# A four-layer attention stack: expert blocks with first weights copied by VectorE and a turned first product, and a third layer on multiplied weights

## The chip, the cores and the metric

The kernel runs on one core of a Trainium2 chip. The core has a matrix engine (TensorE, PE in the profile; PEld is its weight loading), a vector engine (VectorE, DVE), a scalar engine (ScalarE, ACT), GpSimd (POOL) and SyncE (SP), which here only issues transfers. Each engine works through its own instruction stream in order and waits on semaphores for the others. The metric is the time of one execution on the device in microseconds (us), as the median of several runs.

## The reference

Four layers follow each other on 64 sequences of 64 tokens of width 128 (4096 tokens), all in float32: an attention layer with relative positions, an encoder-decoder layer, a "vision" layer, and a layer with two attentions and a mixture of experts. The change touches the last two. Cut to what matters:

```python
# third layer: per sequence, one pooled vision vector gates the tokens
vision_pooled = jnp.mean(vision_feat, axis=1, keepdims=True)
text_proj   = einsum('blh,oh->blo', text_feat, Wt) + bt
vision_proj = einsum('bkh,oh->bko', vision_pooled, Wv) + bv
agreement   = sum(text_proj * vision_proj, axis=-1)
# (third round) weights = softmax over the sequence of 2*agreement
weighted = weights * vision_proj
gate  = sigmoid(text_proj @ Wg_t.T + weighted @ Wg_v.T + bg)
fused = text_feat + gate * weighted          # then a layer norm

# end of the fourth layer: 8 experts, each token goes to its best 2
h = _ln(x, ln_g, ln_b)
vals, idx = top_k(h @ rw.T + rb, 2);  gates = softmax(vals)
h1 = gelu(hf @ fc1_w[e].T + fc1_b[e])        # 128 -> 512
eo = h1 @ fc2_w[e].T + fc2_b[e]              # 512 -> 128
out = x + sum_over_2(gates * eo[idx])
```

## The kernel before, in words

Tokens are worked on in eight groups of 512. The first layer is written with a fixed order of instructions; everything after it (`other_layers`) is a set of Python generators that a small loop, `drive`, advances in turn, so that instructions of several groups are traced interleaved. Behind that stands the library's planner: it takes the traced order as priority and puts on each engine's stream whatever its own timing model holds to be ready first, within the number of buffers of each tile name. An engine then runs its stream strictly in the planned order.

Per group the later layers are `self1`, `cross1`, `forward1`, `layer2` (the vision layer), `self3` and `cross3`. `cross3` ends in `router`: it finds both experts of each token and a row number for each, and writes the normalised row of each token (`zx`, 128 values and four more columns: the token's number, its first expert, and two numbers from which the gate is made) twice into a DRAM table `hrows`, by eight indirect writes of GpSimd per group. Then the router computes the gate-weighted second bias of the experts (tiles `gates`, `pgt`, `T`, and a product with `fc2b`) and adds it to `x`.

`experts` works through that table in blocks of 128 rows of one expert: 47 blocks for the first five groups and 31 for the other three, 78 in all. It is traced beside the last routers, from the point at which the last attention has issued its exponentials, and takes the rest of the program. For block t one round of its loop traces:

- `load(t+6)`: SP reads the row number into a register and loads 128 rows (eight buffers);
- `first(t)`: PE reads the expert's offset into a register; one product of 512 columns with the rows as stationary operand (`f<-fcw,vp` in the profile, two passes); VectorE copies the result out of PSUM (`h<-f`);
- `hidden_turned(t-1)`: four PE transposes (`ht<-ident,h`), then four ScalarE gelus with the bias of the hidden unit as per-partition operand;
- `second(t-3)`: four accumulated products (`f<-fcw,s`, two passes each), VectorE multiplies by the gate (`km<-f,m`), GpSimd scatters the rows to `yrows`;
- `turn(t+2)`: one PE transpose of the loaded rows (`xt`), ScalarE scale and shift (`vp<-xt,cols`), and four one-column VectorE operations for gate and target row (`m`, `tob`).

The buffers that count: six result tiles `you`, sixteen `tob`, four `h1`, seven PSUM banks. When a half is done, `summed` adds the two result rows of each token to `x`: per group one GpSimd addition and one VectorE addition of 128x512, then the store. For five groups this happens among the blocks of the second half, for the last three after the last block.

All instructions go through one helper, so the profile gives line 74 for nearly all; tiles tell them apart.

Of the kernel before, what the change touches and what calls it, by code (L numbers as in the profile page):

```python
# [16 lines left out]
P = 128  # L17
B = 64
S = 64
# [14 lines left out]
ROWW = D + 4  # L34
# [60 lines left out]
def kernel(ctx: ExitStack, tc: tile.TileContext, a: dict, out: bass.AP):  # L95
# [573 lines left out]
    def experts():  # L669
# [7 lines left out]
        def table(h):  # L677
# [11 lines left out]
            for e in range(1, NE):  # L689
# [19 lines left out]
                tab[:, 1, :], eb[0:1, :], float(NE - 1), 1024.0, ALU.min, ALU.mult  # L709
# [28 lines left out]

        def turn(i):
            h, j = slot(i)  # L740
            b = held[i]
            rows_in = b["in"]
            pt = pmm("xt")
            nc.tensor.transpose(pt[:, 0:P], rows_in[:, 0:D], ident)
            b["x"] = wtile([P, P], "vp", 3)
            nc.scalar.activation(b["x"], pt[:, 0:P], AF.Identity, scale=col("moe_g"), bias=col("moe_b"))

            m = wtile([P, 3], "m", 12)
            b["to"] = wtile([P, 1], "tob", 16, U32)
            nc.vector.tensor_tensor(  # L750
                m[:, 0:1], rows_in[:, D + 1 : D + 2], tables[h][1][:, j : j + 1], ALU.is_equal
            )
            nc.vector.tensor_tensor(
                m[:, 2:3], rows_in[:, D + 1 : D + 2], tables[h][1][:, j : j + 1], ALU.not_equal
            )
            nc.vector.tensor_scalar(
                b["to"], m[:, 2:3], float(PARTS[h] * T), rows_in[:, D : D + 1], ALU.mult, ALU.add
            )
            nc.vector.tensor_scalar(
                m[:, 1:2], m[:, 0:1], rows_in[:, D + 3 : D + 4], rows_in[:, D + 2 : D + 3], ALU.mult, ALU.add  # L760
            )
            b["gate"] = m[:, 1:2]

        def first(i):
            h, j = slot(i)
            b = held[i]
            b["e"] = value(nc.tensor, tables[h][0][0:1, 1, j : j + 1], (NE - 1) * 1024)
            ps = pmm("f1")
            nc.tensor.matmul(ps, lhsT=b["x"], rhs=fcw[:, bass.ds(b["e"], 512)], start=True, stop=True)
            b["u"] = wtile([P, 512], "h1", 4)  # L770
            nc.vector.tensor_copy(b["u"], ps)

        def hidden_turned(i):
            h, j = slot(i)
            b = held[i]
            pt = pmm("ht")
            for c in range(NFC):
                nc.tensor.transpose(pt[:, c * P : (c + 1) * P], b["u"][:, c * P : (c + 1) * P], ident)
            b["h"] = wtile([P, 512], "s", 10)
            for c in range(NFC):  # L780
                nc.scalar.activation(
                    b["h"][:, c * P : (c + 1) * P], pt[:, c * P : (c + 1) * P], AF.Gelu,
                    bias=tables[h][2][:, c, j : j + 1],
                )
# [3 lines left out]
        def second(i):  # L788
# [3 lines left out]
            for c in range(NFC):  # L792
                nc.tensor.matmul(
                    po[:, 0:D], lhsT=b["h"][:, c * P : (c + 1) * P],
                    rhs=fcw[:, bass.ds(b["e"] + (512 + c * D), D)],
                    start=(c == 0), stop=(c == NFC - 1),
                )
            y = you[i % 6]
            nc.vector.tensor_scalar(y, po[:, 0:D], b["gate"], None, ALU.mult)
# [24 lines left out]
        def summed(g, ys):  # L824

            o = wtile([P, NBLK, D], "o", 2)
            nc.gpsimd.tensor_tensor(o, ys[0], v3(xs[g][:, :], NBLK), ALU.add)
            nc.vector.tensor_tensor(o, o, ys[1], ALU.add)
            nc.sync.dma_start(out[g * NBLK : (g + 1) * NBLK].rearrange("k p d -> p k d"), o)
# [9 lines left out]
        you = [room[:, 8 * ROWW + k * D : 8 * ROWW + (k + 1) * D] for k in range(6)]  # L839
        total = LAST[-1]  # L840
        reads = {}
        for t in range(-6, total + 3):
# [3 lines left out]
            if h < NH and h not in tables:  # L846
                yield from table(h)
            if t + 6 < total:
                load(t + 6)
            if 0 <= t < total:  # L850
                first(t)
            if 0 <= t - 1 < total:
                hidden_turned(t - 1)
            if 0 <= t - 3 < total:
                second(t - 3)
# [3 lines left out]
            for h in range(NH - 1):  # L859
                gl, at = divmod(t - 3 - LAST[h] - 4, 4)  # L860
                if 0 <= gl < PARTS[h]:
                    g = sum(PARTS[:h]) + gl
                    if at == 0:
                        reads[g] = read(g)
                    if at == 2:
                        summed(g, reads.pop(g))
# [9 lines left out]
    def other_layers(ends):  # L876
# [4 lines left out]
        fc2b = wtile([NE, D], "fc2b", 1)  # L881
# [4 lines left out]
        nc.scalar.dma_start(fc2b, a["fc2b"])  # L886
# [13 lines left out]
        toki = wtile([P, max(PARTS) * NBLK], "toki", 1, I32)  # L900
# [41 lines left out]
        def small_heads(qT, kvT, wq, wk, wv, wo, scale, bias=None, maskb=None, then=None, bare=None, row_behind=None):  # L942
# [147 lines left out]
            scores(1)  # L1090
            yield
            turn_weights(0)
            yield
            turn_weights(1)
            yield
            turn_weights(2)
            products(0)
            yield
# [51 lines left out]

        ff = {}

        def cross1(g):
            x = xs[g]
            if g == 1:
                value_biases()
            if g == 0:
# [11 lines left out]
                bare=lambda: transpose4(ct.rearrange("p b i -> p (b i)")),  # L1169
# [16 lines left out]
        def layer2(g):  # L1186
            x = xs[g]
            load_expert(g)
            ct = ctx_of(g, 2)
            wt, wv, wgt, wgv = (w2l[:, i, :] for i in range(4))  # L1190
            xT = turned(x)
            pool = wtile([P, NB], "pool", 2)
            nc.vector.tensor_reduce(pool, ct, axis=AX.X, op=ALU.add)
            nc.vector.tensor_scalar(pool, pool, 1.0 / S, None, ALU.mult)
            yield
            pv = extra("pv")
            nc.tensor.matmul(pv[0:NB, 0:D], lhsT=pool, rhs=wv, start=True, stop=True)
            vp = wtile([P, D], "vp", 3)[0:NB, :]
            nc.vector.tensor_tensor(vp, pv[0:NB, 0:D], row("l2_bv")[0:NB, :], ALU.add)
            pv2 = extra("pv2")  # L1200
            nc.tensor.matmul(pv2[:, 0:NB], lhsT=wv, rhs=pool, start=True, stop=True)
            vpT = wtile([P, NB], "vpT", 2)
            nc.vector.tensor_scalar(vpT, pv2[:, 0:NB], col("bv"), None, ALU.add)
            ptp = project(xT, wt)
            tpT = wtile([P, T], "T", 4)
            nc.scalar.activation(tpT, ptp, AF.Identity, bias=col("bt"))
            yield

            pa = pmm("pa")
            nc.tensor.matmul(pa[0:NB, :], lhsT=vpT, rhs=tpT, start=True, stop=True)  # L1210
            eye = last(ident[0:NB, 0:NB], S)
            rwd = wtile([NB, NB, S], "rwd", 2)
            nc.vector.tensor_tensor(rwd, v3(pa[0:NB, :], NB), eye, ALU.mult)
# [4 lines left out]
            am = wtile([NB, 2], "am", 2)  # L1218
# [9 lines left out]
            pw = pmm("pw")  # L1228
            nc.tensor.matmul(pw, lhsT=vp, rhs=rw2, start=True, stop=True)
            wvT = wtile([P, T], "T", 4)  # L1230
            nc.scalar.copy(wvT, pw)
            pw2 = pmm("pw2")
            for k in range(NBLK):
                nc.tensor.matmul(
                    pw2[:, k * P : (k + 1) * P], lhsT=rw2[:, k * P : (k + 1) * P], rhs=vp, start=True, stop=True
# [3 lines left out]
            yield  # L1239
            pg = tokens_by(lambda c: (tpT, wvT)[c], lambda c: (wgt, wgv)[c], 2)  # L1240
            gt = wtile([P, T], "z", 3)
            nc.vector.tensor_tensor(v3(gt[:, :], NBLK), v3(pg[:, :], NBLK), mid(row("l2_bg"), NBLK), ALU.add)
# [74 lines left out]
        def router(g, hT, x, zx):  # L1317
# [59 lines left out]
            nc.vector.tensor_tensor(e2, e2, g1, ALU.mult)  # L1377
# [6 lines left out]
            nc.vector.tensor_copy(meta(2), e2)  # L1384
            nc.vector.tensor_tensor(meta(3), g1, e2, ALU.subtract)
# [17 lines left out]
            yield  # L1403

            gates = wtile([P, NBLK, NE], "gates", 3)
            nc.vector.tensor_tensor(gates, hots[0], last(g1[:, :], NE), ALU.mult)
            nc.vector.tensor_tensor(hots[1], hots[1], last(e2[:, :], NE), ALU.mult)
            nc.vector.tensor_tensor(gates, gates, hots[1], ALU.add)
            yield
            pgt = extra("pgt")  # L1410
            for k in range(NBLK):
                nc.tensor.transpose(pgt[0:NE, k * P : (k + 1) * P], gates[:, k, :], ident)
            gT = wtile([NE, T], "T", 4)
            nc.vector.tensor_copy(gT, pgt[0:NE, :])
            yield
            pb = tokens_by(lambda c: gT, lambda c: fc2b)
            nc.vector.tensor_tensor(x, pb, x, ALU.add)

# [26 lines left out]
    fcw = mtile([P, NE * 1024], "fcw")  # L1445

    def load_expert(e):
        nc.scalar.dma_start(fcw[:, e * 1024 : e * 1024 + 512], a["fc1"][e])
        nc.scalar.dma_start(
            v3(fcw[:, e * 1024 + 512 : (e + 1) * 1024], NFC), a["fc2"][e].rearrange("(f c) d -> c f d", c=P)  # L1450
        )
# [87 lines left out]
```

## Time and profile before

| | |
|---|---|
| median of 3 runs (lowest to highest) | 1729.73 us (1729.42 to 1736.37) |
| the profiled execution, its span | 1729.11 us, 1727.3 us |
| busy: PE, PEld, DVE, ACT, POOL | 1589.0, 1148.9, 1209.1, 1002.0, 913.4 us |
| first layer | about 0 to 727 us |
| layers two to four | about 727 to 1513 us |
| expert blocks, first product to last scatter | 1513.2 to 1712.1 us |
| last reads, sums and stores | 1713.5 us to the end |

Engines overlap, so busy times do not add up to the span. "Idle before" an instruction names the engine or transfer that released it. In a line such as `f<-fcw,s 128*128 x8` the output tile stands left of the arrow and the inputs right of it, digits left out; f is any of the tiles f1 and f2.

### The profile page before, as it was taken

The numbers are of one execution on the slowest core, as the hardware profiler recorded it, in microseconds if no ns is written. First come the engines' busy times: TensorE is split into PE (matmuls) and PEld (weight loads), VectorE is DVE, ScalarE is ACT, GpSimd is POOL, SyncE is SP. The second block draws the span as 40 slices with busy tenths as digits, with TensorE's granted clock in tenths as the row PEclk, the third lists the DMA queues.
The fourth block names the chain that finished last, engine by engine and source line by source line (L and its number), as shares of the span: only waits on it lengthen the run. The fifth ranks groups of instructions, "written<-read, shape, count | busy, mean of one in ns | idle before, by whom it ended". The sixth has DMA issues, their size and how long they took to land.

```text
span 1727.3 us, 45290 instructions
## 1 busy us (share of the span) xinstructions
PE 1589.0 (92%) x17528; PEld 1148.9 (67%) x17528; DVE 1209.1 (70%) x3295; ACT 1002.0 (58%) x2744; POOL 913.4 (53%) x875
## 2 busy tenths in 40 slices
PE   6799999999999999879989998899898997799995
PEld 4566666666666666557766776666676676667774
DVE  4567686767676767668887788668756777676663
ACT  4465555555555555447765655657777874146663
POOL 2446374646464655567877676544422343664454
PEclk9899999999999999979999999989998998589998
DMA  6756554555554555340001000000000000122243
GB/s 163 161 137 158 131 135 126 138 131 143 129 144 130 145 146 159 102 123 8 12 24 32 23 20 14 7 8 2 2 14 21 2 14 16 51 72 58 53 125 90
DMA packets 215157, 136.72 MB, mean 79 GB/s; under 512 B 38896, under 2 KB 198786, under 8 KB 214816
## 3 DMA queue, kind: packets, MB, share of 16 engines
q1 hardware_dynamic: 186880, 90.54, 22.2%
q10 hardware_dynamic: 23520, 34.75, 6.1%
q0 software_dynamic: 4544, 8.54, 1.5%
q8 instruction: 140, 2.29, 0.6%
q14 instruction: 73, 0.60, 0.1%
HBM read 66.51 MB, written 68.19 MB: 78 GB/s over the span
## 4 chain that ended last, share of the span: by engine, by line
PE 65%; DVE 17%; ACT 6%; POOL 6%; DMA 3%; issue 2%; SPq 0%; POOLq 0%; ACTq 0%; DVEq 0%
PE av L74 8%; PE psv L74 7%; PE proj L74 7%; PE f L74 6%; PE psk L74 6%; PE pt L74 6%; PE tok L74 5%; DVE mx L74 4%; PE pbd L74 4%; DVE s L74 4%; PE psc L74 3%; PE acc L74 3%; PE tr L74 3%; ACT z L74 2%; PE sc L74 2%
## 5 line engine op out<-in xcount | busy, mean ns | idle before, releaser
L74 ACT ACTIVATE s<-s,nm 128x128 f32<-128x128 f32 x512 | 198.0, 388 | 249.1 <-DVE nm L74 227.3
L74 POOL TENSOR_TENSOR s<-s,sm 128x512 f32<-128x512 f32 x128 | 130.6, 1041 | 252.5 <-DVE sm L74 252.5
L74 PE MATMUL pt<-ident,s 128*128 128x128 f32 x1536 | 213.9, 283 | 27.4 <-DVE s L74 11.3
L74 POOL TENSOR_TENSOR s<-s,mx 128x512 f32<-128x512 f32 x160 | 164.6, 1048 | 99.4 <-DVE mx L74 94.7
L74 PEld LDWEIGHTS pt<-ident,s 128*128 128x128 f32 x1536 | 177.4, 145 | 48.0 <-issue 17.7
L74 ACT ACTIVATE pT<-pt 128x512 f32<-128x512 f32 x256 | 140.7, 601 | 78.1 <-PE pt L74 73.9
L74 POOL TENSOR_TENSOR skew<-skew,mb 128x512 f32<-128x512 f32 x128 | 160.2, 1274 | 38.1 <-DMA skew<-scr 37.6
L74 POOL TENSOR_TENSOR rs<-rs,nhalf 128x4 f32<-128x4 f32 x80 | 81.5, 1020 | 183.8 <-DVE rs L74 155.3
L74 PEld LDWEIGHTS av<-vb,pT 128*64 128x64 f32 x4096 | 132.8, 143 | 22.8 <-issue 12.7
L74 PE MATMUL av<-vb,pT 128*64 128x18 f32 x4096 | 140.8, 216 | 6.2 <-DVE o L74 4.3
L74 DVE TENSOR_REDUCE mx<-s 128x8 f32<-128x512 f32 x160 | 102.8, 675 | 41.6 <-ACT s L74 41.6
L74 PE MATMUL psk<-kv,wk 128*128 128x512 f32 x256 | 128.8, 626 | 0.0
L74 PE MATMUL psv<-wv,kv 128*128 128x256 f32 x512 | 127.4, 392 | 0.0
L74 POOL DMA_INDIRECT yrows<-km,tob x78 | 76.3, 978 | 86.6 <-DVE m L74 62.4
L74 PE MATMUL sc<-km,qs 32*64 32x256 f32 x2048 | 102.9, 414 | 8.8 <-ACT qs L74 4.9
L74 DVE COPY pT<-pt 128x512 f32<-128x512 f32 x128 | 82.1, 682 | 37.3 <-PE pt L74 37.3
L74 PEld LDWEIGHTS psv<-wv,kv 128*128 128x128 f32 x512 | 92.2, 189 | 15.1 <-issue 1.0
L74 PEld LDWEIGHTS pbd<-rT,qp 64*128 64x128 f32 x1024 | 62.3, 187 | 58.3 <-DVE qp L74 56.5
L74 PEld LDWEIGHTS av<-pT,v 128*64 128x64 f32 x2048 | 66.5, 138 | 51.1 <-issue 28.2
L74 DVE TENSOR_TENSOR s<-sc,mb 128x512 f32<-128x512 f32 x128 | 82.4, 680 | 25.0 <-PE sc L74 25.0
L74 DVE TENSOR_TENSOR s<-psc,skew 128x512 f32<-128x512 f32 x128 | 87.4, 683 | 14.8 <-issue 6.5
L74 ACT ACTIVATION_READ_ACCUMULATOR s<-s,nm 128x1 f32 x512 | 95.6, 187 | 0.0
(243 smaller groups left out, 3679.5 us busy)
## 6 DMA issues: line engine op xcount, KB each, us to landing
scr<-stage SPq DMA_DIRECT2D x64, 516.0 KB, 5.3
skew<-scr SPq DMA_DIRECT2D x128, 256.0 KB, 3.9
hrows<-pad ACTq DMA_DIRECT2D x66, 330.0 KB, 2.7
ctx<-in_ctxT SPq DMA_DIRECT2D x24, 256.0 KB, 2.8
km<-hrows SPq DMA_DIRECT2D x78, 66.0 KB, 1.9
fcw<-in_fc ACTq DMA_DIRECT2D x16, 256.0 KB, 3.4
kv<-in_xT SPq DMA_DIRECT2D x8, 256.0 KB, 4.9
kv<-in_ctxT SPq DMA_DIRECT2D x8, 256.0 KB, 8.3
```

What stands on the lines that cost most here:

```text
L74: ins = it(*args, **kw)
```

## The change

**Expert blocks.** VectorE copies the four 128x128 pieces of the block's first weights into a tile (`stage_weights(t+1)`), at an offset that it reads into a register of its own, 78 times. `first` then multiplies with these as stationary operand and the turned rows as moving operand, four products of 128 columns, whose result is already turned: the copy out of PSUM and the four transposes go, and the gelus read the product. `second` follows two rounds behind instead of three. The weights' layout in SBUF changes accordingly. The gate is no longer applied in the block: `second` adds the expert's second bias instead (`fcb`, a 128x1024 table loaded once by a broadcast transfer on SP). The two gate columns of the table rows go (130 columns for 132), and with them two of the four one-column operations.

**Router and sums.** The router stores both gates in a tile `gate` and ends after the scatters: bias product, transposes, copy and addition are gone, for every group. `summed` applies the gates: eight VectorE operations of 128x128 per group in place of one GpSimd and one VectorE operation of 128x512.

**Third layer.** Once, the kernel multiplies Wt and Wg_t together (and bt with Wg_t, into the gate's bias). The pooled vision vector, its projection and that projection times Wt are computed in `cross1`, beside its attention, and kept. `layer2` then works from `xT` directly: the 512-column projection with its ScalarE evacuation, the 512-column product `pw` with its evacuation, the second load of the context and two turns of the generator are gone; a projection of the vision vectors by Wg_v and by bt, and their copies, are new.

```diff
+        def stage_weights(i):
+            h, j = slot(i)
+            b = held[i]
+            b["v"] = value(nc.vector, tables[h][0][0:1, 1, j : j + 1], (NE - 1) * D)
+            b["w"] = wtile([P, NFC, P], "h1", 4)
+            nc.vector.tensor_copy(b["w"], fcw[:, 0:NFC, bass.ds(b["v"], P)])
...
-            m = wtile([P, 3], "m", 12)
+            m = wtile([P, 1], "m", 12)
...
+            nc.vector.tensor_scalar(
+                m, rows_in[:, D + 1 : D + 2], tables[h][1][:, j : j + 1], float(PARTS[h] * T),
+                ALU.not_equal, ALU.mult,
             )
...
+            nc.vector.tensor_tensor(b["to"], m, rows_in[:, D : D + 1], ALU.add)
...
             ps = pmm("f1")
-            nc.tensor.matmul(ps, lhsT=b["x"], rhs=fcw[:, bass.ds(b["e"], 512)], start=True, stop=True)
-            b["u"] = wtile([P, 512], "h1", 4)
-            nc.vector.tensor_copy(b["u"], ps)
-
-        def hidden_turned(i):
...
             for c in range(NFC):
-                nc.tensor.transpose(pt[:, c * P : (c + 1) * P], b["u"][:, c * P : (c + 1) * P], ident)
+                nc.tensor.matmul(
+                    ps[:, c * P : (c + 1) * P], lhsT=b["w"][:, c, :], rhs=b["x"],
+                    start=True, stop=True,
+                )
...
-            nc.vector.tensor_scalar(y, po[:, 0:D], b["gate"], None, ALU.mult)
+            nc.vector.tensor_tensor(y, po[:, 0:D], fcb[:, bass.ds(b["v"], D)], ALU.add)
...
-            nc.gpsimd.tensor_tensor(o, ys[0], v3(xs[g][:, :], NBLK), ALU.add)
-            nc.vector.tensor_tensor(o, o, ys[1], ALU.add)
+            x3 = v3(xs[g][:, :], NBLK)
+            for k in range(NBLK):
+                nc.vector.scalar_tensor_tensor(
+                    o[:, k, :], ys[0][:, k, :], gate[:, g, 0, k : k + 1], x3[:, k, :], op0=ALU.mult, op1=ALU.add
+                )
+                nc.vector.scalar_tensor_tensor(
+                    o[:, k, :], ys[1][:, k, :], gate[:, g, 1, k : k + 1], o[:, k, :], op0=ALU.mult, op1=ALU.add
+                )
...
+            if 0 <= t < total:
+                first(t)
+            if 0 <= t - 2 < total:
+                second(t - 2)
             if t + 6 < total:
                 load(t + 6)
-            if 0 <= t < total:
-                first(t)
-            if 0 <= t - 1 < total:
-                hidden_turned(t - 1)
-            if 0 <= t - 3 < total:
-                second(t - 3)
+            if 0 <= t + 1 < total:
+                stage_weights(t + 1)
             if 0 <= t + 2 < total:
                 turn(t + 2)
...
+        def vision(g, ct):
+            pool, vpT, uT = (visions[:, g, k, :] for k in range(3))
+            nc.vector.tensor_reduce(pool, ct, axis=AX.X, op=ALU.add)
+            nc.vector.tensor_scalar(pool, pool, 1.0 / S, None, ALU.mult)
+            yield
+            pv = pmm("pv")
+            nc.tensor.matmul(pv[:, 0:NB], lhsT=w2l[:, 1, :], rhs=pool, start=True, stop=True)
+            nc.vector.tensor_scalar(vpT, pv[:, 0:NB], col("bv"), None, ALU.add)
...
+            nc.tensor.matmul(pu[:, 0:NB], lhsT=wtn, rhs=vpT, start=True, stop=True)
+            nc.vector.tensor_copy(uT, pu[:, 0:NB])
...
-            ptp = project(xT, wt)
-            tpT = wtile([P, T], "T", 4)
-            nc.scalar.activation(tpT, ptp, AF.Identity, bias=col("bt"))
-            yield
+            nc.tensor.matmul(pv[0:NB, D : 2 * D], lhsT=vpT, rhs=wgv, start=True, stop=True)
+            nc.tensor.matmul(pv[0:NB, 2 * D : 2 * D + 1], lhsT=vpT, rhs=col("bt"), start=True, stop=True)
...
-            pw = pmm("pw")
-            nc.tensor.matmul(pw, lhsT=vp, rhs=rw2, start=True, stop=True)
-            wvT = wtile([P, T], "T", 4)
-            nc.scalar.copy(wvT, pw)
...
-            pg = tokens_by(lambda c: (tpT, wvT)[c], lambda c: (wgt, wgv)[c], 2)
+            pg = tokens_by(lambda c: (xT, rw2)[c], lambda c: (wgx, vp[1])[c], 2)
...
-            gates = wtile([P, NBLK, NE], "gates", 3)
-            nc.vector.tensor_tensor(gates, hots[0], last(g1[:, :], NE), ALU.mult)
-            nc.vector.tensor_tensor(hots[1], hots[1], last(e2[:, :], NE), ALU.mult)
-            nc.vector.tensor_tensor(gates, gates, hots[1], ALU.add)
-            yield
-            pgt = extra("pgt")
-            for k in range(NBLK):
-                nc.tensor.transpose(pgt[0:NE, k * P : (k + 1) * P], gates[:, k, :], ident)
-            gT = wtile([NE, T], "T", 4)
-            nc.vector.tensor_copy(gT, pgt[0:NE, :])
-            yield
-            pb = tokens_by(lambda c: gT, lambda c: fc2b)
-            nc.vector.tensor_tensor(x, pb, x, ALU.add)
```

## The prediction

> **What bounds the kernel now.** I read the table of stretches first (busy time of PE, PEld, DVE, ACT, POOL, then granted clock, DMA share, GB/s). PE fills the expert blocks; between 1450 and 1500 us it is neither full nor at full clock.
>
> ```profile
> 1450.00:1500.00 50.00, 43.44 (x375) 37.32 (x376) 29.52 (x171) 15.29 (x32) 25.01 (x26) 0.64 0.09 30
> 1550.00:1600.00 50.00, 50.00 (x327) 38.57 (x327) 35.31 (x129) 32.30 (x108) 22.99 (x24) 1.00 0.21 59
> ```
>
> Then the timeline (start, duration, engine) of one steady block:
>
> ```profile
> 1600.59 0.60 PE L74 MATMUL ht<-ident,h 128*128 128x128 f32 x4
> 1600.79 0.69 DVE L74 COPY h<-f 128x512 f32<-128x512 f32 x1
> 1601.02 1.06 PE L74 MATMUL f<-fcw,s 128*128 x8
> 1601.92 0.27 PE L74 MATMUL xt<-ident,km 128*128 128x128 f32 x1
> 1602.03 1.02 PE L74 MATMUL f<-fcw,vp 128*128 x2
> 1602.12 0.35 DVE L74 TENSOR_SCALAR km<-f,m 128x128 f32<-128x128 f32 x1 [0.64 <-PE f L74]
> 1602.75 0.98 POOL L74 DMA_INDIRECT yrows<-km,tob  x1 [1.32 <-DVE m L74]
> 1602.89 0.60 PE L74 MATMUL ht<-ident,h 128*128 128x128 f32 x4
> ```
>
> PE goes from start to start without a hole: transposes 0.43, second product 0.90, turn 0.11, first product 0.86, together 2.30 us a block. DVE waits for it. But the first 35 us of the blocks look different: VectorE is stopped by a scatter, and PE by VectorE.
>
> ```profile
> 1540.32 0.21 DVE L74 TENSOR_SCALAR tob<-m,km 128x1 uint32<-128x1 f32 x1 [3.71 <-DMA yrows<-km,tob]
> 1542.99 1.09 PE L74 MATMUL ht<-ident,h 128*128 128x128 f32 x4 [3.32 <-DVE h L74]
> ```
>
> GpSimd is the reason: from 1506 to 1546 it still has 24 scatters of the routers at some 1.27 us from start to start, so blocks' scatters come late. By 1547 only 11 of 78 blocks have had their first product. Third, the chain of waits at the blocks' start:
>
> ```profile
> 1510.25 2.00 PE tok L74 x8
> 1512.25 0.42 PE xt L74
> 1513.21 2.07 PE f L74 x2
> ```
>
> The router's bias product stands just before the first block. Adding up this chain's pieces from 727 to 1513 gives PE 316, DVE 251, ACT 94, POOL 77 us (41, 33, 12, 10%): no engine alone bounds that stage.
>
> **The change part by part.** The sum is made against the profiled 1729.11 us (span 1727.3 and 1.8 around it), 0.6 under the median of 1729.73.
>
> *Blocks, PE.* The four transposes (0.43) go. The first product becomes four pairs of a 128-column weight load and product, like the second one, which takes 0.90 for four; so 0.90 for 0.86. New period 0.90 + 0.90 + 0.11 = 1.91 us, 0.39 less. In the first blocks (11, and two more that a faster PE may fit in) GpSimd sets the pace and its scatters are unchanged, so I count 65 blocks: −25.4. Bounds: 0 if something else holds 2.30, −30.4 if all 78 gain.
>
> *Blocks, VectorE.* Gone: the PSUM copy (0.69), the gate (0.35), four small operations. New per block: the weight copy, SBUF to SBUF, 128x512; nearest row `z<-z`, 0.36 at its fastest, bounded above by the 0.69 of the PSUM copy. The bias addition, as the 128x128 addition `obias<-pob,rows`, 0.29; mask and target row 0.20 and 0.15 (`tob`, `m`). A register load, never seen on DVE: on PE's queue it takes 0.30, on SP's 0.27; address arithmetic for two moving operands, 0.07 each by SP's rows (37 and 29 ns).
>
> ```profile
> L329 PEldq TENSOR_LOAD <-table x78: 296/302/482, 1511.2 to 1702.2; - x78
> L74 DVE TENSOR_SCALAR z<-z x8: 364/412/1562, 1001.0 to 1212.9; 128x512 f32<-128x512 f32 x8
> ```
>
> Laid end to end: 0.36 + 0.29 + 0.20 + 0.15 + 0.30 + 0.14 = 1.44 us (1.77 with the slow copy), below 1.91. ACT stays at 1.14 of gelus and 0.46 of scaling, POOL at 1.28 a scatter, SP at its load: all fit. The new wait is PE's on the weight copy. If VectorE copied in traced order, the copy for t+1 would queue behind the bias addition that waits for `second(t-2)`, and PE would idle. I take this as hidden, because the planner sends ready VectorE work ahead. Counts up to 1600 us:
>
> ```profile
> L74 DVE TENSOR_SCALAR m<-m,km 128x1 f32<-128x1 f32 x41 | 10.9, 267 | 0.0
> L74 PE MATMUL xt<-ident,km 128*128 128x128 f32 x35 | 10.2, 296 | 0.0
> ```
>
> A block's small operations and its `xt` are traced in the same round, yet VectorE is six blocks ahead. A copy needs only the table and a free one of four buffers, so it can run up to three ahead.
>
> *A rule against the copy.* Small SBUF-only operations on VectorE are stretched exactly until a GpSimd addition ends (first pair), but not inside a GpSimd scatter (second pair):
>
> ```profile
> 1171.05 1.35 DVE L74 TENSOR_SCALAR ag<-ag,am 8x64 f32<-8x64 f32 x1
> 1171.09 1.27 POOL L74 TENSOR_TENSOR x<-x,obias 128x512 f32<-128x512 f32 x1 [1.27 <-ACT z L74]
> ...
> 1506.91 0.95 POOL L74 DMA_INDIRECT hrows<-zx,to  x1 [0.30 <-issue]
> 1507.63 0.20 DVE L74 TENSOR_SCALAR g<-e 128x4 f32<-128x4 f32 x1
> ```
>
> So I take no blocking by scatters. If a copy did wait out a whole scatter (0.98), the serial sum would be 2.42 and the period no better than before; that is rival 2. [...]
>
> *Routers.* Per group PE loses four transposes and eight products, DVE some 2 us. No such product lies before 1447; four groups' lie between 1447 and 1506, four after. On the chain from 1447 to 1513 I count 1.01 + 0.85 + 0.85 of `pgt` and 1.08 + 1.08 + 1.85 + 1.15 + 2.00 of bias products: 9.9 us. What is late next is VectorE's router work, whose pieces stand between; I take −8 (bounds −12 and 0). The four later groups fall where GpSimd holds the pace: 0.
>
> *Third layer.* PE loses two 512-column products a group, each like the first product (0.86), and gains one 128-column pair (0.22) and two tiny ones (0.1 each by estimate from the pair): −1.3. ACT loses 0.69 and 0.58. DVE gains three small evacuations, 0.28 + 0.21 + 0.15. Times eight, −10.4, −10.2 and +5.2. Weighted with the chain's shares: −4.3 − 1.2 + 1.7 = −3.8. One of the eight context loads that go lay on the chain with 2.65 us; a third of it makes −5 in all. Bounds: −20 if both engines' savings count in full, +6 if only DVE's additions do. The one-time products of weights are some 1 us and lie beside the first `cross1`.
>
> *Sums.* Per group eight DVE operations with one per-partition scalar, 0.29 (`obias`) to 0.35 (`km<-f,m`), so 2.3 to 2.8, for 0.69 on DVE and 1.31 on POOL. At the end the first sum starts at 1716.93; groups end 2.55 apart, the third after the first store frees its buffer (3.03 after that store's issue in the old rows): 1716.93 + 2.55 + 3.03 + 2.55 = 1725.1 for 1723.96: +1 (0.6 to 1.6). For the five earlier groups DVE gets 1.6 more per four blocks, 0.4 a block, which with 1.44 comes to 1.84 of 1.91: some blocks lose a little, +2 (0 to 6).
>
> *Free:* the broadcast of `fcb` (512 KB on SP) can go as soon as the last attention's keys are read, about 1447, and row loads begin at 1507; without that cover it costs some 5 us, as a 516 KB transfer here lands after 5.3. Narrower rows: nothing. First layer: untouched.
>
> Sum: −25.4 − 8 − 5 + 1 + 2 = −35, so 1729.1 − 35 = 1694 us.
>
> **Rivals.**
> 1. *More is kept.* The third layer saves its 20, the routers 12, all 78 blocks their 0.39: −20 − 12 − 30 + 3 gives 1670. For it speaks that the chain before the blocks is nearly all PE; against it the 33% of DVE and the pace of GpSimd early.
> [...]
> 3. *Slower: the weight copy is planned just in time, behind the bias addition.* Then PE waits after each second product for addition, load and copy: 0.1 + 0.29 + 0.30 + 0.36 and 0.1 of semaphore, less the 0.11 turn, about 1.05, and the period is near 3.0. 65 blocks × 0.7 = +45 on the others' −10: 1764. It decides from a period of about 2.45 (65 × 0.15 eats the 10). For: the traced order asks for t+1 only. Against: the six-block lead.
> 4. *The new order of the attention stage happens to be worse* (VectorE twice stood 5 us before a router's write in the old one): +10 on my sum, 1704, inside the range.
>
> **How the numbers follow.** My forecast 0.62, with its own range 1680 to 1708 (its bounds for layer three, routers and sums, rival 4 in it); rival 1 0.12; rival 2 0.14; rival 3 0.12. The range reaches over rivals 1 and 2: 1667 to 1722. A difference under 0.5%, 8.6 us, is about what a measurement here cannot tell from none: faster is below 1721, slower above 1738. Rival 2 falls a half on each side of 1721: faster 0.62 + 0.12 + 0.08 = 0.82, same 0.06, slower 0.12.
>
> **What would show it.** Right: PE starts of successive blocks 1.9 us apart from some 1550 on, no hole on PE in front of `f`, weight copies of 0.35 to 0.45 running two or more blocks ahead of their product, and the first block some 13 us earlier. Wrong: PE's idle time before `f` released by the DVE copy (rival 3); copies of about 1 us ending with a scatter (rival 2); a stage 727 to 1500 of the same length (layer three kept nothing). The sum is most exposed in the number of blocks that GpSimd paces, each worth 0.39, and in the planner's order.

## The result, and the profile after

The changed kernel takes 1703.7 us (median of 4 runs, 1702.3 to 1706.9) beside 1730.3 for the kernel before (four runs by then): a ratio of 0.984, 95% interval 0.982 to 0.987, or 27 us less. The profiled execution took 1706.88 us (span 1705.0), the slowest of the four; of before it took 1729.11. Three places tell where the time went. They are read off these two profiled executions, whose spans differ by 22.3 us: −40.0 + 16.9 + 0.8.

First the blocks. In the steady timeline (start, duration, engine) the first product `f<-vp,h` starts every 1.9 us:

```profile
1599.17 0.43 DVE L74 COPY h<-fcw 128x512 f32 x1 [0.62 <-PE f L74]
1599.89 1.06 PE L74 MATMUL f<-vp,h 128*128 128x128 f32 x8
1600.79 1.06 PE L74 MATMUL f<-fcw,s 128*128 x8
1600.92 0.28 DVE L74 TENSOR_TENSOR km<-f,km 128x128 f32<-128x128 f32 x1
1601.48 0.98 POOL L74 DMA_INDIRECT yrows<-km,tob  x1 [1.74 <-DVE tob L74]
1601.53 0.43 DVE L74 COPY h<-fcw 128x512 f32 x1 [0.26 <-issue]
1601.68 0.27 PE L74 MATMUL xt<-ident,km 128*128 128x128 f32 x1
1601.79 1.06 PE L74 MATMUL f<-vp,h 128*128 128x128 f32 x8
```

PE has no hole: 0.90 from the first product to the second, 0.89 from there to the turn `xt`, 0.11 to the next first product. From the first block's product to the last block's scatter it is now 1530.1 to 1688.0, 157.9 us, where it was 1513.2 to 1711.1, 197.9. That is 40 us less, and not the 25 of the forecast.

Second, the first block starts 17 us *later* than before, where the forecast had it 13 us earlier. Laid beside before's, the stretches show the loss only from about 970 on, in the groups' third layers, and with it a lower granted clock (columns: busy time of PE, PEld, DVE, ACT, POOL; then clock, DMA share, GB/s). Of before:

```profile
970.00:1260.00 290.00, 265.45 (x3220) 193.19 (x3220) 214.63 (x591) 179.84 (x368) 152.25 (x133) 0.95 0.03 10
```

and of after:

```profile
970.00:1260.00 290.00, 268.61 (x2944) 196.48 (x2950) 196.78 (x584) 159.72 (x331) 153.63 (x133) 0.86 0.02 5
```

PE is as busy as before, but gets through fewer instructions in the same time, at 0.86 of the clock. By groups of instructions between 975 and 1240 (busy time, mean ns of one), before had

```profile
L74 PE MATMUL tok<-w2l,T 128*128 128x128 f32 x128 | 17.0, 280 | 0.1
```

for the eight gate products, and after has

```profile
L74 PE MATMUL tok<-vg,rwd 8*128 8x128 f32 x64 | 21.0, 419 | 0.0
L74 PE MATMUL tok<-w2l,T 128*128 128x128 f32 x64 | 20.5, 413 | 0.0
```

The number of products is the same, and so are their 128 columns. The two rows of after overlap and so can't be added: measured from the start of each gate product to its end, the eight take 37.5 us in after and 17.0 in before. Half of the products contract 8 rows (the 8 sequences' weights, `rwd`, with the vectors `vg`) in place of 128. These products stood in no step of the prediction.

So the stretch in which before had 0.64 of the clock and the first bias products, 1450 to 1500, still belongs to the attention in after, and PE fills the blocks from 1600 on (same columns):

```profile
1450.00:1500.00 50.00, 43.11 (x563) 39.11 (x561) 28.75 (x137) 19.44 (x39) 20.73 (x21) 0.74 0.07 23
1600.00:1650.00 50.00, 50.00 (x447) 49.67 (x446) 25.03 (x109) 38.60 (x129) 24.61 (x25) 1.00 0.37 102
```

In front of the first block no bias product stands any more; PE waits there for VectorE's router work and then, last, for the rows that GpSimd's scatters wrote (timeline, PE alone):

```profile
1527.41 0.61 PE L74 MATMUL pr<-both,tri 128*128 128x32 f32 x2 [2.44 <-DVE before L74]
...
1529.09 1.03 PE L74 MATMUL xt<-ident,km 128*128 128x128 f32 x2 [0.64 <-DMA km<-hrows]
1530.11 2.08 PE L74 MATMUL f<-vp,h 128*128 128x128 f32 x8
```

Third, the tail: from the last scatter's start to the end of the span it is 17.0 us for 16.2.

### The profile page after: what moved, and what is told of

The parts are those of the page before. It is cut to its first block, busy times and chain, and to the rows that moved or that the text cites. A ratio compares the mean times of both kernels' runs of the same rounds, so it can differ in the third digit from the quotient of the medians.

```text
span 1705.0 us, 45485 instructions
## 1 busy us (share of the span) xinstructions
PE 1565.4 (92%) x17609; PEld 1167.1 (68%) x17609; DVE 1158.2 (68%) x3175; ACT 994.2 (58%) x2728; POOL 905.7 (53%) x867
## 4 chain that ended last, share of the span: by engine, by line
PE 67%; DVE 16%; ACT 5%; POOL 5%; DMA 4%; issue 2%; SPq 0%; POOLq 0%; ACTq 0%; DVEq 0%
PE proj L74 8%; PE av L74 8%; PE psv L74 7%; PE f L74 7%; PE pt L74 7%; PE psk L74 6%; PE tok L74 6%; PE pbd L74 4%; DVE mx L74 4%; PE psc L74 3%; DVE s L74 3%; PE acc L74 3%; PE tr L74 3%; PE sc L74 2%; ACT z L74 2%
```

## The experiments

When the first of them were chosen, three accounts of the 17 us stood: A, the 8-row gate products (I thought of the clock); B, the planner's new order of the attention stage; C, something outside the third layer, in the shortened routers or the blocks traced beside them.

**The third layer of before, all else changed.**

```diff
         def layer2(g):
...
-            wv, wgv = w2l[:, 1, :], w2l[:, 3, :]
...
+            ct = ctx_of(g, 2)
+            wt, wv, wgt, wgv = (w2l[:, i, :] for i in range(4))
...
-            pg = tokens_by(lambda c: (xT, rw2)[c], lambda c: (wgx, vp[1])[c], 2)
+            pg = tokens_by(lambda c: (tpT, wvT)[c], lambda c: (wgt, wgv)[c], 2)
```

> The changed kernel with the third layer of before (own context load, projection of the tokens, 128-row gate products); expert blocks, routers and sums as changed. The first block started at 1513.2 before and at 1530.1 after. Theory A (the third layer lost those 17 us and more, because its new gate products with 8 contracted rows hold the granted clock down between 970 and 1240) and theory B (the third layer lost them, because the planner laid out the attention stage in a worse order around it) both expect the first block at 1505 (1513 less the routers' 8) to 1513 and a time of 1675 to 1690. Rival C (the third layer is innocent; the loss comes from the shorter routers or the blocks traced beside the last groups) expects the first block near 1530 and 1700 to 1710.

Measured: 1690.8 us (ratio 0.977, interval 0.974 to 0.979), first block at 1513.5, clock between 970 and 1260 back at 0.95. C falls: the new third layer costs 1703.7 − 1690.8 = 13 us in the changed kernel. The time lies a little above A's and B's range, because the first block stands where it stood before: the routers' 8 us did not show there.

**The new third layer alone, on the kernel before.**

> The kernel before with the third layer's change alone (weights multiplied, vision vectors in cross1, gate products with 8 rows); the token numbers' integer tile shares another buffer, to make room. Theories A and B expect a loss of 15 to 30 us, 1745 to 1760, all of it before the first block. Theory A also expects granted clocks of 0.55 to 0.85 in several stretches of 10 us between 1000 and 1240, where before had 1.00 nearly throughout; theory B expects the loss without the clock's fall, as idle time of PE. My predicted term of -5 expects 1725, rival C 1722 to 1732.

Measured: 1746.9 us, ratio 1.010 (1.008 to 1.012), 16.6 us slower, first block at 1532.7 (19.5 later), clock between 970 and 1260 at 0.86. The term of −5 is refuted in sign.

**Full rows in the gate product.** The second factor stands in tiles of 128 rows whose other 120 are zeros, written once:

```diff
+        gw8 = [wtile([P, NB, S], f"gw8{k}", 1) for k in range(2)]
+        vg8 = [wtile([P, D], f"vg8{k}", 1) for k in range(2)]
+        for t8 in gw8 + vg8:
+            nc.gpsimd.memset(t8, 0.0)
...
-            pg = tokens_by(lambda c: (xT, rw2)[c], lambda c: (wgx, vp[1])[c], 2)
+            r128 = gw8[g % 2].rearrange("p b l -> p (b l)")
+            pg = tokens_by(lambda c: (xT, r128)[c], lambda c: (wgx, vg8[g % 2])[c], 2)
```

> The changed kernel, but the gate product's second factor (weights of a token and vg) stands in tiles of 128 rows with 120 rows of zeros, written once, so that these products contract 128 rows and not 8: same number of instructions, same columns, same result. Theory A expects the granted clock between 1000 and 1240 back at 0.95 or more, the first block 15 to 25 us earlier (1505 to 1515) and 1680 to 1690. Theory B expects the same as after, 1699 to 1709, with the clock as low as in after.

Measured: 1686.3 us (ratio 0.975, 0.973 to 0.977), 17.4 below after; first block at 1508.6. The streams of PE, VectorE and ScalarE have the same instructions in the same order as after's, and GpSimd's has four memsets more: so it is not the order, and B falls as the cause of these 17 us. But A in its first form, in which the clock alone costs the time, does not hold either: the clock came back to 0.91 only, where A expected 0.95, and the products are shorter *at the same clock*. One gate product of after, at a clock of 0.98 (timeline, PE alone):

```profile
1118.07 0.49 PE L74 MATMUL tok<-w2l,T 128*128 128x128 f32 x2
1118.49 0.48 PE L74 MATMUL tok<-vg,rwd 8*128 8x128 f32 x2
1118.90 0.49 PE L74 MATMUL tok<-w2l,T 128*128 128x128 f32 x2
1119.32 0.48 PE L74 MATMUL tok<-vg,rwd 8*128 8x128 f32 x2
```

and the same of this run, at 1.00:

```profile
1105.90 0.49 PE L74 MATMUL tok<-w2l,T 128*128 128x128 f32 x2
1106.23 0.39 PE L74 MATMUL tok<-vg,gw 128*128 128x128 f32 x2
1106.45 0.39 PE L74 MATMUL tok<-w2l,T 128*128 128x128 f32 x2
1106.68 0.39 PE L74 MATMUL tok<-vg,gw 128*128 128x128 f32 x2
```

From start to start of a pair of passes: 0.42 us where the row count changes, 0.22 where it stays (the first pair of this run stands behind the 8-row product `pw` and takes 0.33). The weight loads show where the difference lies. The load for the second pair above (timeline, PEld), first of after, then of this run:

```profile
1118.48 0.29 PEld L74 LDWEIGHTS tok<-vg,rwd 8*128 8x128 f32 x2
...
1106.12 0.30 PEld L74 LDWEIGHTS tok<-vg,gw 128*128 128x128 f32 x2
```

With equal rows the load starts 0.11 us ahead of its product (1106.12 and 1106.23), under the product in front of it; where the row count changes it starts only 0.01 ahead (1118.48 and 1118.49). The stretches of whole gate products (length, PE busy, PEld busy, ..., clock) show the same. Of after, at 0.98 and at half clock:

```profile
1118.07:1121.46 3.39, 3.39 (x18) 2.42 (x17) 3.39 (x12) 0.59 (x1) 1.86 (x2) 0.98 0.02 5
1054.25:1060.10 5.85, 5.85 (x18) 4.06 (x18) 1.99 (x13) 0.59 (x1) 2.91 (x3) 0.50 0.00 0
```

and with full rows:

```profile
1105.90:1107.96 2.06, 2.06 (x18) 2.06 (x18) 2.06 (x9) 0.59 (x1) 0.54 (x1) 1.00 0.03 8
1194.98:1198.77 3.79, 3.79 (x19) 3.79 (x19) 2.11 (x9) 2.60 (x6) 2.75 (x3) 0.50 0.00 0
```

PEld fills the whole stretch with equal rows (2.06 of 2.06 us) and 70% of it with alternating ones (2.42 of 3.39, 4.06 of 5.85). That gave a new theory: a *change* of the row count costs, not the 8 rows as such and not the clock alone.

**The two turns of the generator put back.**

```diff
+            yield
             pa = pmm("pa")
...
+            yield
             pg = tokens_by(lambda c: (xT, rw2)[c], lambda c: (wgx, vp[1])[c], 2)
```

> The changed kernel with the two turns of the generator put back in layer2 (one ahead of the agreement product, one ahead of the gate product): not an operation more or less, only the traced order, and with it the planned order. Theory A expects no more than 5 us either way, 1699 to 1709, with the clock low where gate products stand. Theory B expects more than 5 us, and earlier if the missing turns are what made the order worse: 1680 to 1697.

Measured: 1703.4 us, but its four runs lay between 1690.5 and 1712.4, at mean granted clocks of 0.939 down to 0.929. The median does not differ from after's, as A had it; with that spread the run decides nothing on effects under 10 us. It shows something else: one and the same order can end 22 us apart, the longer runs at the lower clock.

**Half as many changes of rows.** Every second pair is turned round:

```diff
-            pg = tokens_by(lambda c: (xT, rw2)[c], lambda c: (wgx, vp[1])[c], 2)
+            pg = pmm("tok")
+            for k in range(NBLK):
+                ks = slice(k * P, (k + 1) * P)
+                pair = [(xT, wgx), (rw2, vp[1])]
+                for c, (l, r) in enumerate(pair[::-1] if k % 2 else pair):
+                    nc.tensor.matmul(pg[:, ks], lhsT=l[:, ks], rhs=r, start=(c == 0), stop=(c == 1))
```

> The changed kernel; in the gate product every second pair is turned round (128-row, 8-row, 8-row, 128-row, ...), so that its row count changes 4 or 5 times in place of 8; same products, same row counts, all else in the same order. The gate product took 3.3 us at full clock and 5.85 at half clock in after, 2.05 and 3.79 with 128 rows throughout. If changing between 8 and 128 rows is what costs (switch theory), about half of that difference goes: some 2.7 us at full clock, 4.8 at half, and 5 to 10 us of the whole: 1694 to 1699. If a product of 8 rows is itself slow (row theory), nothing changes: 3.3 and 5.85, and 1701 to 1707.

Measured: 1697.4 us, 6.3 below after (ratio 0.982, 0.979 to 0.984, beside 0.984); on the chip of this run the kernel before took 1730.8, within 0.5 of the others so far. Its gate products:

```profile
1112.50:1115.33 2.83, 2.83 (x18) 2.35 (x18) 1.05 (x8) 0.59 (x1) 0.00 (x0) 1.00 0.02 6
1181.94:1186.92 4.98, 4.98 (x18) 4.08 (x18) 0.00 (x0) 1.36 (x3) 0.00 (x0) 0.50 0.00 0
```

So 2.83 and 4.98, beside 2.7 and 4.8 expected by the switch theory and 3.3 and 5.85 by the row theory. The stretches also give the price. Inside the stretch, after has 7 changes of rows more than the run with full rows, and this one 4 more (the one on entry, from the 8-row product `pw`, all three have). At full clock (0.98 in after) that is (3.39 − 2.06) / 7 = 0.19 us and (2.83 − 2.06) / 4 = 0.19 us a change; at half clock (5.85 − 3.79) / 7 = 0.29 and (4.98 − 3.79) / 4 = 0.30.

**64 and 72 rows.** As with full rows, but the products take only the first 64, or the first 72, rows of the padded tiles:

```diff
-            pg = tokens_by(lambda c: (xT, r128)[c], lambda c: (wgx, vg8[g % 2])[c], 2)
+            pg = tokens_by(lambda c: (xT, r128[0:64, :])[c], lambda c: (wgx, vg8[g % 2][0:64, :])[c], 2)
```

> The run with full rows (1686.3 us), but the gate product's second factors contract the first 64 rows of the padded tiles (56 of them zeros). Any-difference theory (every change of the row count costs): as with 8 rows, the gate product takes 3.3 us at full clock and 5.85 at half, 1699 to 1707. Step theory (TensorE runs in a few fixed heights, 128 among them, and only a change of height costs): the same if 64 rows are a height of their own, and 2.05, 3.79 and 1684 to 1689 if they run at the height of 128. Idle-rows theory (the cost grows with the rows that do nothing): about half way, 2.7, 4.8 and 1693 to 1698. [...]

> The same with 72 rows. Any-difference theory: 3.3 us at full clock, 5.85 at half, 1699 to 1707. Step theory with a step at 64: 2.05, 3.79 and 1684 to 1689, as with 128 rows. Idle-rows theory: close to the run with 64 rows, a little under it. [...]

These two and the next ran on another chip, on which the kernel before took 1764.5 us; they are compared with each other and with that. Measured: 1748.6 us with 64 rows, 1728.1 with 72 (ratios 0.991, interval 0.988 to 0.994, and 0.981, 0.976 to 0.985): 20.5 us between them. In the profiled executions the first blocks lie 16.6 us apart (1549.4 and 1532.8). Both ratios are worse than those of the runs with 8 and with 128 rows (0.984 and 0.975), though the gate products are alike: on this chip PE also stood in front of the blocks' products waiting for turned rows (`vp`), 9.8 us with 64 rows and 16.0 with 72, and not at all in after. What held those rows up was not found. A gate product at full and at half clock with 64 rows:

```profile
1113.21:1116.60 3.39, 3.39 (x18) 2.42 (x17) 2.23 (x10) 0.59 (x1) 0.53 (x1) 1.00 0.02 5
1207.11:1212.97 5.86, 5.86 (x18) 4.07 (x18) 3.96 (x13) 2.60 (x6) 4.80 (x5) 0.50 0.00 0
```

and with 72:

```profile
1109.03:1111.09 2.06, 2.06 (x18) 2.06 (x18) 2.06 (x9) 0.59 (x1) 0.54 (x1) 1.00 0.03 8
1198.12:1201.91 3.79, 3.79 (x18) 3.79 (x18) 2.08 (x9) 2.60 (x6) 2.79 (x3) 0.50 0.00 0
```

64 rows cost to the hundredth what 8 cost (3.39 us; at half clock 5.86 beside 5.85), 72 what 128 cost (2.06 and 3.79). Any-difference and idle-rows theories both fall; a step between 64 and 72 stands: 0.19 us at each change between 8 or 64 and 128 rows, (3.39 − 2.06) / 7, and none between 72 and 128. Of the step theory the runs show this one step and no more. No gate product here alternates between 8 and 64 rows, so what a change between those two costs was not shown.

**The third layer alone, with full rows in the gate product, on the kernel before** (the edit of the third run on the kernel of the second).

> The kernel before with the third layer's change alone, as in the run of 1746.9 us, but with the gate product's second factors in 128-row tiles. If the rows explain the whole loss, the third layer is worth here what it is worth beside the new blocks (1686.3 - 1690.8 = -4.5): 1725 to 1727; my term was -5. If the new traced order of the third layer costs something besides, 1730 or more. The difference to 1746.9 is expected at 17 to 21 us, as from the changed kernel (17.4).

Measured: 1759.8 us beside 1764.5: −4.7, ratio 0.998 (0.996 to 1.0004). The size agrees with the −4.5 expected, though the interval still holds no change. The difference to the kernel of 1746.9 us can't be taken across chips; by ratios it is 1.0099 − 0.9982, 1.2% or 20 us, as expected.

**All third-layer products full.** The four products `pw` ahead of the gate product get 128 rows too:

```diff
-            vp = [wtile([P, D], "vp", 3)[0:NB, :], vg8[g % 2][0:NB, :]]
+            vp = [vp8[g % 2][0:NB, :], vg8[g % 2][0:NB, :]]
...
-                    pw2[:, k * P : (k + 1) * P], lhsT=rw2[:, k * P : (k + 1) * P], rhs=vp[0], start=True, stop=True
+                    pw2[:, k * P : (k + 1) * P], lhsT=r128[:, k * P : (k + 1) * P], rhs=vp8[g % 2], start=True, stop=True
```

> The run with full rows (gate product from 128-row tiles with 120 zero rows), and the four products of the weighted vision vectors ahead of it (8 rows each, as in the kernel before) get 128 rows in the same way. Switch theory: those four have 8 rows all alike, so only one change of rows at each end goes, 0.2 to 0.3 us a group: 1682 to 1687 beside 1686.3. If any product with 8 rows pulls the granted clock down, the half clock that stood at 1011 to 1021 and 1164 to 1178 goes, some 10 us of lost clock: 1676 to 1681.

Measured: 1682.0 us (ratio 0.972, 0.970 to 0.974), the fastest kernel of the study: 48 below before, 22 below after. It lies at the lower end of what the switch theory gives and a little above the other. The clock is what is new:

```profile
970.00:1260.00 290.00, 265.39 (x3414) 206.19 (x3414) 216.81 (x637) 181.41 (x372) 161.10 (x139) 0.94 0.02 6
```

0.94, against 0.91 with only the gate product full; six of the eight gate products now run at full clock, where it was four. Side by side:

| | sum of the 8 gate products, us | clock 970 to 1260 | median, us |
|---|---|---|---|
| after | 37.5 | 0.86 | 1703.7 |
| half the changes | 32.5 | 0.85 | 1697.4 |
| gate product full | 23.2 | 0.91 | 1686.3 |
| all full | 17.2 | 0.94 | 1682.0 |

The product's own length gives most of the first two steps (5.0 of 6.3, and 14.3 of 17.4); in the last it shrinks by 6.0, and the time by 4.3. But that length has the clock in it: by an estimate from the 1.33 us between 3.39 and 2.06, at full clock throughout the seven changes would cost the eight products 8 × 1.33 = 10.6 us, and most of the rest of the 20.3 between after and all full comes of the stretches at lower clock. Why the clock falls is not settled: with half the changes gone it had not moved (0.85 for 0.86).

**The blocks alone, on the kernel before**: copied weights and turned first product; gates stay in the table rows and in the block, routers, sums and third layer as before.

> The kernel before with the turned first product and the copied first weights alone; routers with their bias products, gates in the table rows and in the blocks, sums and third layer as before. My forecast for this part is -25.4 (65 blocks by 0.39): 1705; if all 78 gain 0.39, 1700. The run with the old third layer, which has the shorter routers and the sums besides, took 1690.8; if those are worth the -8 + 3 of my sum, this one takes about 1696; if they are worth nothing, 1691; if the routers' whole 12 counts, 1700 or more. The first block starts at 1513 (as in before) and the block stage, 198 us in before and 158 in after, takes 158 to 172.

Measured: 1700.4 us, ratio 0.983 (0.981 to 0.985): −30, which is all 78 blocks by 0.39. The block stage takes 164.9 us (1513.5 to 1678.4). With the shorter routers and the gates in the sums it is 1690.8, so these two are worth some −10 together, and the stage 158.2. The first block starts at 1513.5 in both runs, beside 1513.2 in before.

## Why the prediction was right or wrong

The time, 1703.7, lies inside 1667 to 1722 and inside the forecast's own 1680 to 1708; the sign was right. That the time came so near is in part luck: the forecast of 1694 missed by only 10, because one term was wrong by 18 and the two others, each 5 too small, made up for 10 of it; the rest is rounding and the difference between the two times of before.

| term | predicted, us | measured, us |
|---|---|---|
| blocks | −25.4 | −30 |
| routers, and all sums | −8 + 1 + 2 | −10 |
| third layer | −5 (−20 to +6) | +13 (+16.6 alone on before) |
| sum | −35 | −27 |

**Blocks, PE:** right in mechanism and size: 0.90 + 0.89 + 0.11 = 1.90 for the 1.91 forecast. **The 65 blocks** were wrong; all 78 gain, as rival 1 had it. I took GpSimd's scatters to set the pace until 1546. Before, VectorE's wait for a scatter (3.71 us at 1540.32) reached PE through the copy out of PSUM (3.32 us at 1542.99). After, PE needs of VectorE a weight copy made ahead, and the reading of the second product (`km`) that frees its PSUM bank; the pace is 1.9 us from the fourth block on, while GpSimd still scatters for the routers (last at 1556.7). All that is left of the pacing is one hole before a product in 78 blocks, 3.1 us behind such a `km`, as the answer on tile `f` of after shows:

```profile
L74 PE MATMUL f<-vp,h x624: 275/275/582, 1530.1 to 1683.6; 128*128 128x128 f32 x156
...
  DVE km L74: 3.1, 1
```

I had counted what a resource paces under the old dependencies, and the change removed the dependency.

**Blocks, VectorE:** the copy takes 0.43 and not 0.36; VectorE is busy for 25 of the 50 us from 1600 to 1650, so this costs nothing. Rival 3 (copy just in time) did not come about: by 1600 us 38 copies had started for some 34 first products, so the planner does send them ahead, as the counts of before had let me hope. Rival 3's 0.1 of semaphore was an estimate; in before PE's transposes at 1542.99 start 0.05 us after the copy that they wait for, and ScalarE's scaling at 1602.29 starts 0.10 after the turn. Rival 2 (copy held by the scatter, the blocks' 25 lost, 1719) neither: the copy at 1601.53 in the timeline above lies wholly inside the scatter of 1601.48 and takes 0.43. So do all 47 copies that lie wholly inside a scatter, and the six that touch none; the longest of the 78 took 0.67. The row of before, 0.20 us for a small operation inside a scatter of 0.95, had pointed that way.

**Routers:** size about right, place wrong. I took 9.9 us of bias products off a chain of PE's. In the run with the old third layer they are gone, and PE stands idle there instead, waiting for the router's normalised rows (timeline, PE):

```profile
1488.42 0.61 PE L74 MATMUL pr<-both,ones 128*128 128x32 f32 x2
1497.98 1.63 PE L74 MATMUL tr<-ident,zx 128*128 128x128 f32 x4 [8.94 <-ACT zx L74]
```

ScalarE writes those rows, and it waits for its turn at the buffer, which an earlier scatter of GpSimd still reads (timeline, ACT):

```profile
1497.43 1.65 ACT L74 ACTIVATE zx<-x,nmr,rs 128x128 f32<-128x128 f32 x4 [11.95 <-DMA hrows<-zx,to]
```

So where the bias products had stood there is now a wait for GpSimd. What the routers' change did give comes later: their last scatter is at 1539.1 with the old third layer, 1546.3 with blocks alone, and the block stage is 6.7 us shorter. The step "What is late next is VectorE's router work" named the wrong engine: in that run the chain that ends at the first block runs through the landing of a scatter (1507.59, 2.34 us) and the load of the rows (1511.11, 2.12 us), and GpSimd issues these scatters back to back, 1.27 us apart.

**Third layer:** this is the step that failed. Of its sum, "PE loses two 512-column products a group ... and gains one 128-column pair ... and two tiny ones", the count is right, and the result with full rows, 1686.3 − 1690.8 = −4.5, agrees with the −5 predicted. What it left out is that the eight gate products keep their number and columns but not their rows: it put their change at nothing, without a reason. They went from 17.0 to 37.5 us, because half of them contract 8 rows beside 128 and each change of rows costs 0.19 us at full clock and 0.29 to 0.30 at half, and because the clock was lower there (0.86 for 0.95). The bound of +6 was too narrow for the same reason: it looked only at what VectorE gains. Of the prediction's own signs of being wrong, the one on the stage from 727 to 1500 came true, and beyond: the stage did not keep its length, it grew by 17 us.

**Rival 4** gave 1704, and that is the time, but its mechanism (a worse order) is not what happened: with the same order on PE, VectorE and ScalarE, and 128 rows, the kernel takes 1686. That it met the time to the microsecond is chance.

**Sums:** 0.35 us for each of the 64 operations and a tail longer by 0.8, as forecast.

**Two slips of arithmetic** in the prediction change nothing: 8 × 0.64 is 5.1 and not 5.2, and with half of rival 2's 0.14 on each side of 1721 the chance of faster adds up to 0.81 and not 0.82.

## What to carry to other kernels

When a product is replaced by one with fewer contracted rows, look at its neighbours on TensorE: here a stream that alternated between 128 rows and 8 or 64 paid 0.19 us at each change at full clock, nearly twice a 128-column pass, of which two take 0.22, while products padded with zero rows took no longer than full ones (0.22 for both). So pad the small operand with zero rows to 128 (1686.3 us for 1703.7 here), or put products with the same row count side by side (1697.4 with half of the changes). Where a resource seems to set the pace, name the dependency by which it does, and ask whether the change leaves that dependency standing. And before a removed operation is counted as a gain on a chain, ask what its engine will wait for instead.

## What was not expected of the hardware

- Contracting 64 rows beside 128 costs to the hundredth what 8 rows beside 128 cost (3.39 us for the gate product, at a clock of 1.00 and 0.98), and 72 rows what 128 cost (2.06 at 1.00).
- The granted clock falls to 0.50 in stretches where PE shows as busy throughout, as in the stretch of after from 1054.25 to 1060.10 (PE 5.85 of 5.85; the ends of products are modelled in the profile, so short gaps could be hidden). From 970 to 1260 it was 0.86 with alternating rows, 0.85 with half the changes, 0.91 with the gate product full and 0.94 with all rows full. What lowers it was not shown.
- The kernel with the two turns put back, one and the same order in all four runs, ended between 1690.5 and 1712.4 at mean clocks of 0.939 to 0.929, while after itself stayed within 4.5 us.
